# Two-layer attention kernel: softmax sums of one block interleaved with the folds of the block ahead

## Chip, cores, metric

The kernel runs on one core of a Trainium2 chip. The metric is device time in microseconds from start to end of the program. The engines are TensorE (PE, matrix products), VectorE (DVE), ScalarE (ACT), GpSimd (POOL) and SyncE (SP). Each has its own queue of instructions. SP and POOL also issue DMAs; a DMA that adds into its destination is issued from POOL.

## The reference

The input `x` is 16 images of 256 channels on 32 x 32 points, float32. Two layers with the same form run one after the other:

```python
def _conv_ref(x, Wq, bq, Wk, bk, Wv, bv, rel_h, rel_w):
    xf = x.reshape(b, c, n)                     # n = 1024, 4 heads of d = 64
    q, k, v = proj(Wq, bq), proj(Wk, bk), proj(Wv, bv)
    sim = jnp.einsum('bhdi,bhdj->bhij', q, k)
    rel = (rel_h + rel_w).reshape(heads, d, n)
    qpos = jnp.einsum('hdi,bhdj->bhij', rel, q)
    attn = jax.nn.softmax(sim + qpos, axis=-1)
    out = jnp.einsum('bhdn,bhmn->bhdm', v, attn)
    return out.reshape(b, c, w, h)

x = x + _conv_ref(_gn(x), *layer0)              # _gn: mean and variance over groups of the
x = x + _conv_ref(_gn(x), *layer1)              # last axis, 16 groups per image
```

## The kernel before

**Units and blocks.** A unit is one image in one layer; there are 32. A unit has four blocks: two pairs of heads (`pr`), and for each two halves of 512 columns (`half`). Blocks are numbered n = 0 to 127, and b = n mod 4 is called the position of a block in its unit here. `block(n)` issues positions 1 and 2, `block_with_q` position 0, `block_with_values` position 3, and `block_without_pieces` the last two blocks of all. The order of every instruction is written out by hand (`manual_schedule`); each engine takes its own instructions in that order.

**Inside a block.** A block has eight tiles of scores, j = 0 to 7. `seed` (VectorE, L442) writes the positional term into a PSUM tile, `scores` (TensorE, L478) adds the products of `k` and `q`, ScalarE takes the exponential into a tile `p` in SBUF (L487). There are four PSUM tiles (`ring`), one of which serves other products, and so a seed waits for the exponential that frees its tile. `attend` (L532) multiplies the eight `p` tiles with the values in two passes; the first score tile of the next block is computed between the passes. `take_out` (L594, ScalarE) copies the result at the end of each block. Beside this, every block carries pieces of the next unit's work: projections, values, positional terms and the normalisation.

**Normalisation.** `norms` spreads it over a unit in ScalarE activations per group: sums (`SUMS`) and squares for the unit two ahead, and the application (`norm_apply`, L248, from `APPLY`) for the next unit. The application starts in position 0. It needs `rstd` and `nshift`, which GpSimd computes (L237, L239) after VectorE has written `var` (L235) in position 3.

**The chain of softmax sums.** The denominator is the sum over all rows of the eight `p` tiles. For each block:

1. `add_up` (VectorE, L517 and L519) adds tiles 0 to 5 into `acc`, 128 x 1024. There are three `acc` buffers and ten `p` buffers.
2. `add_last` (GpSimd DMA, L550) adds tiles 6 and 7 in the next block: these 512 KB transfers are called chunks here. In position 2, VectorE adds tile 6 of the previous block itself.
3. `fold` (GpSimd DMA, L555) adds the lower half of the partitions to the upper.
4. `stack_up` (SP DMA, L569) copies 32 of the 64 rows into `stack`, and `fold_again` (GpSimd DMA, L574) adds the other 32. Two blocks with two heads each share one stack.
5. `fold_stack` (GpSimd DMA, L579) halves a stack five times: with D = 64, R = 32, R/2, R/4 and R/8 rows.
6. `spread_sums` (SP DMA, L587, four of them) brings the sums to `den_all`; `reciprocals` (VectorE, L629) inverts them and sends them through DRAM (L631, L636) to `rden`.
7. `normalise` (VectorE, L644) multiplies the block pair's result, and `add_by_dma` (GpSimd DMA, L662) adds it to `x`. `store` (SP, L667) writes `x` out after layer 1.

Before the change, steps 2 to 4 of block n-1 all run within block n, in series: each step waits for the DMA ahead of it. Steps 5 to 7 of a pair are spread over the blocks after it. In GpSimd's queue `fold_again` of position 2 stands, in position 3, ahead of `rstd`.

Of the kernel before, what the change touches and what calls it, by code (L numbers as in the profile page):

```python
# [13 lines left out]
ALU = mybir.AluOpType  # L14
# [5 lines left out]
G = 16  # L20
# [32 lines left out]
def fast_path(ctx, tc, sh, x, layers, out, W, den_all, good, flag):  # L53
# [26 lines left out]
    nc = tc.nc  # L80
# [464 lines left out]
    R = P // 4  # L545
    stacks = {}

    def add_last(blk, j0=NT - 1):
        for j in range(j0, NT):
            nc.gpsimd.dma_start(accs[blk], probs[blk, j], accum_op=ALU.add)  # L550

    def fold(blk):

        acc = accs[blk]
        nc.gpsimd.dma_start(acc[:D], acc[D:], accum_op=ALU.add)  # L555
# [20 lines left out]
    def fold_stack(u, pr, rows_):  # L576

        stack = stacks[u, pr]
        nc.gpsimd.dma_start(stack[:rows_], stack[rows_ : 2 * rows_], accum_op=ALU.add)  # L579
# [155 lines left out]


    APPLY = {0: (0, 1, 5, 9, 9), 1: (9, 9, 9, 11, G)}
    SUMS = {0: (0, 0, 0, 1, 7), 1: (7, 9, 11, G, G)}
    SQUARES = {2: (0, 0, 5, 11, G)}

    FIRST_SQUARES = {0: (3, 5, 9, G, G)}
# [2 lines left out]
    def norms(u, b, i):  # L744
# [9 lines left out]
        if u + 2 < NU:  # L754
            norm_squares(u + 2, groups(SQUARES))

    def block(n):
        blk = blocks[n]
        u, b = divmod(n, BPU)
        pr_, half = blk[1:]  # L760

        stacked = blocks[n - 3][:2] if half == 1 and n > 2 else None
        summed = blocks[n - 4][:2] if half == 0 and n > 3 else None
        last_unit = u + 1 == NU
        before = blocks[n - 5][:2] if b == 1 and n > 4 else None
# [8 lines left out]
        folded = n - 1 < FOLDED  # L774
# [7 lines left out]
        if previous and folded and b == 1:  # L782
            add_last(previous, NT - 2)
        elif previous:
            add_up(previous, 6)
            if folded:
                add_last(previous)
            else:
                add_up(previous, 7)
# [12 lines left out]
        add_up(blk, 1)  # L802
        if before:
            reciprocals(*before)
        norms(u, b, 1)
        second(0)
        if half == 1:
            second_out()
        if stacked:
            fold_stack(*stacked, D)  # L810
        if summed:
            fold_stack(*summed, R // 8)
            spread_sums(*summed)
        if previous and folded:
            fold(previous)
        if stacked:
            fold_stack(*stacked, R)
        first(1)
        first_out()
        seed(blk, 5, f0)  # L820
        scores(blk, 5)
        if previous and folded:
            stack_up(previous)
        if b == 2 and n > 5:
            store(*blocks[n - 6][:2])
        add_up(blk, 2)
# [32 lines left out]
        if stacked:  # L859
            fold_stack(*stacked, R // 2)  # L860
        if previous and folded:
            fold_again(previous)
        if half == 1 and u + 3 < NU and units[u + 3][1] == 0 and u > 0 or n == 3:
            load_x(units[u + 3][0], range(pr_, pr_ + 1) if u > 0 else range(CC))
        add_up(blk, 5)
        if n in (2, 6):
            W.mix(n // 4)
        if before and last_unit:
            finish(*before)
        if two and half == 1 or n == 0:  # L870
            mean_out()
        if stacked:
            fold_stack(*stacked, R // 4)
            if n == len(blocks) - 3:
                fold_stack(*stacked, R // 8)
                spread_sums(*stacked)
        if after:
            for j in range(1, 4):
                seed(after, j, ring[j % 3])
        if before and not last_unit:  # L880
            normalise(*before)
            add_by_dma(*before)
        norms(u, b, 3)
        values_of_p(1)
        take_out(blk, po)
        pos[n] = po

    def block_with_q(n):

        blk = blocks[n]  # L890
        u = blk[0]
        r0, r1, r2, r3 = ring
        previous, after, summed = blocks[n - 1], blocks[n + 1], blocks[n - 4][:2]
        folded = n - 1 < FOLDED
        before = blocks[n - 6][:2] if n > 5 else None
        add_last(previous, NT - 2)
# [11 lines left out]
        fold_stack(*summed, R // 8)  # L908
        spread_sums(*summed)
        fold(previous)  # L910
        first(1)
        first_out()
        seed(blk, 6, r0)
        scores(blk, 6)
        stack_up(previous)
        seed(blk, 7, r1)
        scores(blk, 7)
        add_up(blk, 2)
        add_up(blk, 3)
        seed(after, 0, r2)  # L920
        add_up(blk, 4)
        if n in check:
# [6 lines left out]
        fold_again(previous)  # L929
        ring[:] = r2, r0, r1, r3  # L930
        seed(after, 1, r0)
        seed(after, 2, r1)
        add_up(blk, 5)
        seed(after, 3, r2)
        if before:
            store(*before)
        norms(u, 0, 3)
        values_of_p(1)
        take_out(blk, po)
        pos[n] = po  # L940

    def block_with_values(n):
# [1 line left out]
        blk = blocks[n]  # L944
        u = blk[0]
        r0, r1, r2, r3 = ring
        previous, after, stacked = blocks[n - 1], blocks[n + 1], blocks[n - 3][:2]
        before = blocks[n - 5][:2] if n > 4 else None
        two = u + 2 < NU
        v = Values(u + 1, psum2(r3, f"pw_{u + 1}"))  # L950

        add_last(previous, NT - 2)
        scores(blk, 1)
        add_up(blk, 1)
        one = v.half(1, HI, False), v.half(1, LO, True)
# [13 lines left out]
        v.keep(1, 0, 1.0)  # L969
        seed(blk, 5, r2)  # L970
        scores(blk, 5)
        if before:
            reciprocals(*before)
        seed(blk, 6, r1)
        scores(blk, 6)
        v.combine(0, 0, ALU.add)
        fold_stack(*stacked, D)
        fold(previous)
# [5 lines left out]
        fold_stack(*stacked, R)  # L984
        stack_up(previous)
        add_up(blk, 2)
        seed(after, 0, r1)
        v.combine(1, 1, ALU.subtract)
# [12 lines left out]
        scores(after, 0)  # L1001
        v.pair("4", 3, 4, 1)
        v.keep(0, 1, -1.0)
        fold_stack(*stacked, R // 2)
        fold_again(previous)
        if u + 3 < NU and units[u + 3][1] == 0:
            load_x(units[u + 3][0], range(1, 2) if u > 0 else range(CC))
        add_up(blk, 4)
# [1 line left out]
            mean_out()  # L1010
        ring[:] = r1, r0, r3, r2
        seed(after, 1, r0)
        if before:
            normalise(*before)
        v.combine(1, 0, ALU.add)
        fold_stack(*stacked, R // 4)
        seed(after, 2, r3)
        if before:
            add_by_dma(*before)
        add_up(blk, 5)  # L1020
        seed(after, 3, r1)
        values_of_p(1)
# [517 lines left out]
```

## Time and profile before

| | us |
|---|---|
| median of 3 runs | 2757.56 (2753.45 to 2761.12) |
| profiled execution | 2760.36, span 2758.6 |
| granted TensorE clock, mean | 0.972 |
| VectorE adds into `acc` (L519), 550 | 669.7 |
| VectorE seeds (L442), 1018 | 1230.4, idle before them 322.2, of that 287.0 for exponentials |
| GpSimd chunk DMAs (L550), 217 of 512 KB | 6.0 median from issue to landing |
| GpSimd `stack<-acc` (L574) waiting for SP's `stack<-acc` | 422.2 |
| ScalarE exponentials waiting for a chunk DMA, 33 times | 51.4 |

A row of the profile's groups gives line, engine, operation, what is written from what, shape and count; then busy time and the mean of one in ns; then how long the engine stood idle just before such instructions, and which instruction ended most of that. In a timeline the columns are start, length, engine, line and operation, and in brackets the idle time before it. The granted clock is that of TensorE as a share of full speed. Matrix products are pipelined, so that a busy TensorE may still run slowly.

### The profile page before, as it was taken

The page shows a single profiled execution, that of the slowest core. Times are in us where ns is not written, and L with a number is a line of the kernel's source. Part 1 is how long each engine was busy: PE and PEld are TensorE (multiplying, and loading weights), DVE is VectorE, ACT ScalarE, POOL GpSimd, SP SyncE. Part 2 cuts the span into 40 slices and gives each one's busy share as a digit, 9 for nine tenths or more (in the row PEclk, how much of TensorE's full clock was granted, in tenths as well). Part 3 has the DMA queues.
Part 4 walks back from the last instruction along what each step waited for, and adds up shares of the span by engine and source line. Part 5 has one row for each costly group of instructions (what it writes and reads, how often), then busy time and mean ns, then how long its engine had stood idle before and what let it go on. Part 6 is the DMA issues. An engine that isn't in the chain of part 4 may idle for free. (4 is left out here: it accounts for less than half of the span.)

```text
span 2758.6 us, 94006 instructions
## 1 busy us (share of the span) xinstructions
PE 2599.2 (94%) x41192; PEld 1424.4 (52%) x41192; DVE 2233.9 (81%) x2184; ACT 2012.0 (73%) x3977; POOL 937.2 (34%) x1029
## 2 busy tenths in 40 slices
PE   8999999999999999999999999999999999999997
PEld 4555445554455554555545555445554455544554
DVE  7888777887877888788887788887887877878887
ACT  7877767778777786777776778777777776777653
POOL 1333333333333333333233332333323333333330
PEclk9999999999999999999999999999999999999999
DMA  3455555565556555655555556565556555555553
GB/s 95 92 99 107 103 103 107 109 132 115 114 113 120 105 111 108 119 110 113 120 103 114 108 109 117 109 124 114 113 120 118 109 104 108 108 98 109 109 109 83
DMA packets 141906, 302.32 MB, mean 110 GB/s; under 512 B 56361, under 2 KB 57897, under 8 KB 141489
## 3 DMA queue, kind: packets, MB, share of 16 engines
q0 software_dynamic: 75744, 210.33, 44.0%
q1 hardware_dynamic: 65744, 85.90, 11.2%
q8 instruction: 326, 5.34, 0.8%
q14 instruction: 92, 0.75, 0.1%
HBM read 51.78 MB, written 17.30 MB: 25 GB/s over the span
## 5 line engine op out<-in xcount | busy, mean ns | idle before, releaser
L442 DVE TENSOR_TENSOR ps<-abt 128x1024 f32<-128x1024 f32 x1018 | 1230.4, 1227 | 322.2 <-ACT p L487 287.0
L487 ACT ACTIVATE p<-ps,shift 128x1024 f32<-128x1024 f32 x993 | 1067.9, 1111 | 412.6 <-PE ps L478 355.4
L478 PE MATMUL ps<-q,k 64*64 64x512 f32 x7944 | 1003.6, 600 | 111.5 <-DVE ps L442 106.6
L532 PE MATMUL po<-p,v 64*64 64x256 f32 x16384 | 990.1, 390 | 26.5 <-ACT q L279 25.3
L532 PEld LDWEIGHTS po<-p,v 64*64 64x64 f32 x16384 | 661.2, 138 | 382.7 <-issue 91.4
L519 DVE TENSOR_TENSOR acc<-acc,p 128x1024 f32<-128x1024 f32 x550 | 669.7, 1218 | 4.8 <-ACT p L487 2.3
L478 PEld LDWEIGHTS ps<-q,k 64*64 64x64 f32 x7944 | 289.1, 133 | 521.8 <-DVE ps L442 259.8
L550 POOL DMA_DIRECT2D acc<-p x217 | 269.6, 1242 | 543.8 <-DMA acc<-p 219.2
L579 POOL DMA_DIRECT2D stack<-stack x310 | 301.8, 974 | 221.4 <-DMA stack<-stack 186.6
L574 POOL DMA_DIRECT2D stack<-acc x248 | 214.2, 985 | 454.7 <-DMA stack<-acc 422.2
L248 ACT ACTIVATE xn<-x,nshift,rstd 128x128 f32<-128x128 f32 x496 | 208.8, 493 | 132.8 <-POOL nshift L239 132.8
L555 POOL DMA_DIRECT2D acc<-acc x124 | 102.7, 828 | 508.7 <-DMA acc<-p 508.7
L268 PE MATMUL pk<-xn,Wk 64*64 64x512 f32 x2048 | 243.9, 592 | 0.0
L268 PE MATMUL pq<-xn,Wq 64*64 64x512 f32 x2048 | 242.8, 589 | 0.0
L517 DVE TENSOR_TENSOR acc<-p,p 128x1024 f32<-128x1024 f32 x128 | 156.7, 1224 | 92.5 <-ACT p L487 92.5
L190 ACT ACTIVATE junk<-x,neg 128x128 f32<-128x128 f32 x505 | 198.0, 400 | 0.0
L594 ACT COPY od<-po 128x512 f32<-128x512 f32 x127 | 74.2, 584 | 134.1 <-PE po L532 134.1
L268 PEld LDWEIGHTS pq<-xn,Wq 64*64 64x64 f32 x2048 | 77.8, 133 | 142.5 <-issue 133.8
L190 ACT ACTIVATE junk<-x 128x128 f32<-128x128 f32 x464 | 140.0, 310 | 0.0
L268 PEld LDWEIGHTS pk<-xn,Wk 64*64 64x64 f32 x2048 | 74.2, 134 | 125.3 <-issue 123.3
L363 PEld LDWEIGHTS pw<-mixed,t 64*64 64x64 f32 x2976 | 114.3, 133 | 38.3 <-DVE v L405 20.4
L363 PE MATMUL pw<-Wv,xn 64*64 64x128 f32 x1984 | 133.6, 273 | 0.3 <-issue 0.3
(96 smaller groups left out, 1932.3 us busy)
## 6 DMA issues: line engine op xcount, KB each, us to landing
acc<-p POOLq DMA_DIRECT2D x217, 512.0 KB, 6.0
rden<-rd SPq DMA_DIRECT2D x126, 256.0 KB, 4.8
acc<-acc POOLq DMA_DIRECT2D x124, 256.0 KB, 3.5
x<-od POOLq DMA_DIRECT2D x61, 512.0 KB, 4.9
x<-in_x_dram SPq DMA_DIRECT2D x32, 512.0 KB, 4.0
stack<-acc SPq DMA_DIRECT2D x248, 64.0 KB, 2.1
stack<-acc POOLq DMA_DIRECT2D x248, 64.0 KB, 2.9
out_dram<-x SPq DMA_DIRECT2D x31, 512.0 KB, 3.0
```

Of the source, the lines that this page charges most:

```text
L190: nc.scalar.activation(junk, grouped(xt[units[u][0]], g), func, accum_out=into[:, g : g + 1], **bias)
L248: nc.scalar.activation(grouped(xns[u], g), grouped(xt[units[u][0]], g), AF.Identity, bias=shift[:, g : g + 1], scale=rstd[:, g : g + 1],)
L268: yield nc.tensor.matmul(pk[c, nh, :], w[l][rs, cc, c0 : c0 + D], xns[u][rs, cc, nh * HALF : (nh + 1) * HALF], start=(t == 0 and cc == 0), ...
L363: yield nc.tensor.matmul(self.pw[c, a, part * P : (part + 1) * P], x[rs, j0 : j0 + D], w[rs, :], start=first and not whole and part == 0, ...
L442: nc.vector.tensor_tensor(ps.rearrange("p h (w y) -> p h w y", y=H), ab[:, :, :H].unsqueeze(2).to_broadcast([P, 2, XH, H]), ab[:, :, H + h ...
L478: nc.tensor.matmul(ps[c, h, :], a[hs, j0 : j0 + D], b[hs, columns], start=bool(tag) and i == 0, stop=i == len(terms) - 1, skip_group_check ...
L487: nc.scalar.activation(p, ps, AF.Exp, bias=W.shift)
L519: nc.vector.tensor_tensor(accs[blk], accs[blk], probs[blk, j], ALU.add)
L532: yield nc.tensor.matmul(po[c, a, :QUART], vts[u][rs, pr, j, h * D : (h + 1) * D], p[rs, h, a * QUART : (a + 1) * QUART], start=(t == 0 an ...
L550: nc.gpsimd.dma_start(accs[blk], probs[blk, j], accum_op=ALU.add)
L574: nc.gpsimd.dma_start(at, acc[R:D, h, :], accum_op=ALU.add)
L579: nc.gpsimd.dma_start(stack[:rows_], stack[rows_ : 2 * rows_], accum_op=ALU.add)
```

## The change

The sums of a block now take two blocks instead of one. A new function `denominators(n, i)` holds all steps of the chain, in slots i = 0 to 4 of a block, and the three kinds of block call it. In block n the chunks of block n-1 are added, while the folds (steps 3 and 4) are those of block n-2, and the stack and the spread come a block later than before. The chunks of tiles 6 and 7 are now added by DMA in every position, and VectorE no longer adds tile 6 in position 2. For positions 0 and 2, VectorE's add of tile 5 moves to the start of the next block. `reciprocals` moves from before seed 5 to before seed 6 in position 1, and from before seed 6 to after seed 7 in position 3. `normalise` and `add_by_dma` move from the end of positions 1 and 3 to the start of positions 2 and 0 (`residual`). `store` stays in positions 0 and 2, now behind the residual of the same block. One group of `SUMS` moves from the third to the fourth slot of position 0. The order on TensorE is the same as before.

```diff
-    def add_last(blk, j0=NT - 1):
-        for j in range(j0, NT):
-            nc.gpsimd.dma_start(accs[blk], probs[blk, j], accum_op=ALU.add)
+    def add_chunk(blk, j):
+        nc.gpsimd.dma_start(accs[blk], probs[blk, j], accum_op=ALU.add)
...
-    SUMS = {0: (0, 0, 0, 1, 7), 1: (7, 9, 11, G, G)}
+    SUMS = {0: (0, 0, 0, 0, 7), 1: (7, 9, 11, G, G)}
...
+    def denominators(n, i):
+
+        half, end = n % 2, n == FOLDED
+        if n > FOLDED + 1:
+            return
+        previous, older = blocks[n - 1], blocks[n - 2]
+        folding = n <= FOLDED and n > 1
+        stacked = blocks[n - 4][:2] if half == 0 and n > 3 else None
+        summed = blocks[n - 5][:2] if half == 1 and n > 4 else None
+        late = blocks[n - 3][:2] if n == FOLDED + 1 else None
+        if i == 0:
+            if n > 0 and n % BPU in (1, 3):
+                add_up(previous, 5)
+            if end or n > FOLDED:
+                add_up(previous, 6)
+            if n > FOLDED:
+                add_up(previous, 7)
+            elif n > 0:
+                add_chunk(previous, 7 if end else 6)
+            if summed:
+                fold_stack(*summed, R // 8)
+                spread_sums(*summed)
+            if stacked:
+                fold_stack(*stacked, D)
+            if folding:
+                fold(older)
+        elif i == 1:
+            if late:
+                fold_stack(*late, D)
+            if stacked:
+                fold_stack(*stacked, R)
+            if n > 0 and n < FOLDED:
+                add_chunk(previous, 7)
+            elif end:
+                fold(previous)
+            if folding:
+                stack_up(older)
+                fold_again(older)
+        elif i == 2:
+            if late:
+                fold_stack(*late, R)
+            if summed:
+                reciprocals(*summed)
+            if stacked:
+                fold_stack(*stacked, R // 2)
...
+        elif i == 3:
...
+            if stacked:
+                fold_stack(*stacked, R // 4)
...
+    def residual(n):
+        if n > 5:
+            normalise(*blocks[n - 6][:2])
+            add_by_dma(*blocks[n - 6][:2])
...
     def block(n):
...
+        denominators(n, 0)
+        if b == 2:
+            residual(n)
...
         add_up(blk, 1)
-        if before:
-            reciprocals(*before)
...
         seed(blk, 5, f0)
         scores(blk, 5)
-        if previous and folded:
-            stack_up(previous)
+        add_up(blk, 2)
+        denominators(n, 2)
...
     def block_with_q(n):
...
-        add_last(previous, NT - 2)
+        after = blocks[n + 1]
+        denominators(n, 0)
+        residual(n)
...
     def block_with_values(n):
...
-        stack_up(previous)
+        denominators(n, 2)
         add_up(blk, 2)
```

`FOLDED` is 124, the number of blocks whose sums go this way; the last four are treated apart (`end`, `late`), some of their sums staying on VectorE and TensorE.

More of the change, by code (lines that the diff above doesn't have):

```diff
@@ L755, in norms @@
             norm_squares(u + 2, groups(SQUARES))
+    def denominators(n, i):
[42 more added lines that the diff above has]
+                fold_stack(*stacked, R // 2)
+            if end:
+                stack_up(previous)
+        elif i == 3:
+            if late:
+                fold_stack(*late, R // 2)
+            if stacked:
+                fold_stack(*stacked, R // 4)
+            if end:
+                fold_again(previous)
+        elif late:
+            fold_stack(*late, R // 4)
+            fold_stack(*late, R // 8)
+            spread_sums(*late)
+    def residual(n):
+        if n > 5:
+            normalise(*blocks[n - 6][:2])
+            add_by_dma(*blocks[n - 6][:2])
     def block(n):
@@ L760, in block @@
         pr_, half = blk[1:]
-        stacked = blocks[n - 3][:2] if half == 1 and n > 2 else None
-        summed = blocks[n - 4][:2] if half == 0 and n > 3 else None
         last_unit = u + 1 == NU
-        before = blocks[n - 5][:2] if b == 1 and n > 4 else None
         after = blocks[n + 1] if n + 1 < len(blocks) else None
@@ L773, in block @@
         f0, f1, f2, f3 = ring
-        folded = n - 1 < FOLDED
         if not pieces:
@@ L780, in block @@
             return block_with_values(n)
-        if previous and folded and b == 1:
-            add_last(previous, NT - 2)
[L784 to L789, printed above, removed]
+        denominators(n, 0)
+        if b == 2:
+            residual(n)
         if b == 2:
@@ L808, in block @@
             second_out()
[L809 to L813, printed above, removed]
-        if previous and folded:
-            fold(previous)
-        if stacked:
-            fold_stack(*stacked, R)
+        denominators(n, 1)
         first(1)
@@ L821, in block @@
         scores(blk, 5)
-        if previous and folded:
-            stack_up(previous)
+        add_up(blk, 2)
+        denominators(n, 2)
         if b == 2 and n > 5:
             store(*blocks[n - 6][:2])
-        add_up(blk, 2)
         if b == 2:
@@ L858, in block @@
             mean_out = norm_var(1, filled(f1, f"pm_{n}", EPS / 2))
[L859 to L862, printed above, removed]
+        denominators(n, 3)
         if half == 1 and u + 3 < NU and units[u + 3][1] == 0 and u > 0 or n == 3:
             load_x(units[u + 3][0], range(pr_, pr_ + 1) if u > 0 else range(CC))
-        add_up(blk, 5)
+        if b == 1:
+            add_up(blk, 5)
         if n in (2, 6):
             W.mix(n // 4)
-        if before and last_unit:
-            finish(*before)
         if two and half == 1 or n == 0:
             mean_out()
[L872 to L876, printed above, removed]
+        denominators(n, 4)
         if after:
@@ L879, in block @@
                 seed(after, j, ring[j % 3])
-        if before and not last_unit:
-            normalise(*before)
-            add_by_dma(*before)
+        if b == 1 and last_unit:
+            finish(*blocks[n - 5][:2])
         norms(u, b, 3)
@@ L892, in block_with_q @@
         r0, r1, r2, r3 = ring
[L893 to L896, printed above, removed]
+        after = blocks[n + 1]
+        denominators(n, 0)
+        residual(n)
         for j in range(1, 4):
@@ L907, in block_with_q @@
         add_up(blk, 1)
-        fold_stack(*summed, R // 8)
-        spread_sums(*summed)
-        fold(previous)
+        denominators(n, 1)
         first(1)
@@ L928, in block_with_q @@
         scores(after, 0)
-        fold_again(previous)
+        denominators(n, 3)
         ring[:] = r2, r0, r1, r3
[L931 to L936, printed above, removed]
+        for j in range(1, 4):
+            seed(after, j, ring[j % 3])
+        if n > 5:
+            store(*blocks[n - 6][:2])
         norms(u, 0, 3)
@@ L946, in block_with_values @@
         r0, r1, r2, r3 = ring
-        previous, after, stacked = blocks[n - 1], blocks[n + 1], blocks[n - 3][:2]
-        before = blocks[n - 5][:2] if n > 4 else None
+        after = blocks[n + 1]
         two = u + 2 < NU
         v = Values(u + 1, psum2(r3, f"pw_{u + 1}"))
-        add_last(previous, NT - 2)
+        denominators(n, 0)
         scores(blk, 1)
@@ L971, in block_with_values @@
         scores(blk, 5)
-        if before:
-            reciprocals(*before)
         seed(blk, 6, r1)
@@ L976, in block_with_values @@
         v.combine(0, 0, ALU.add)
-        fold_stack(*stacked, D)
-        fold(previous)
+        denominators(n, 1)
         v.pair("3", 5, 7, 0)
@@ L983, in block_with_values @@
         v.keep(1, 1, -1.0)
-        fold_stack(*stacked, R)
-        stack_up(previous)
+        denominators(n, 2)
         add_up(blk, 2)
@@ L1003, in block_with_values @@
         v.keep(0, 1, -1.0)
-        fold_stack(*stacked, R // 2)
-        fold_again(previous)
+        denominators(n, 3)
         if u + 3 < NU and units[u + 3][1] == 0:
@@ L1012, in block_with_values @@
         seed(after, 1, r0)
-        if before:
-            normalise(*before)
         v.combine(1, 0, ALU.add)
-        fold_stack(*stacked, R // 4)
         seed(after, 2, r3)
-        if before:
-            add_by_dma(*before)
         add_up(blk, 5)
```

## The prediction

> **Where the time goes now.** I read the busy shares first, then the groups for who waits for whom, then block by block, then one block in order of time. The page's first part:
>
> ```profile
> PE 2599.2 (94%) x41192; PEld 1424.4 (52%) x41192; DVE 2233.9 (81%) x2184; ACT 2012.0 (73%) x3977; POOL 937.2 (34%) x1029
> ```
>
> TensorE is busy 94% of the span, 159 us short of all of it. But "busy" hides slow products, and the groups say where to look:
>
> ```profile
> L478 PE MATMUL ps<-q,k 64*64 64x512 f32 x7944 | 1003.6, 600 | 111.5 <-DVE ps L442 106.6
> L248 ACT ACTIVATE xn<-x,nshift,rstd 128x128 f32<-128x128 f32 x496 | 208.8, 493 | 132.8 <-POOL nshift L239 132.8
> ```
>
> PE waits almost only for score seeds from VectorE (106.6 us). ScalarE waits 132.8 us for GpSimd's `nshift`, in 29 waits, one per unit. To see whether these are one thing I cut the span at the ScalarE copies that end each block (L594) and took busy time and granted clock of such stretches. First come blocks 48 to 51 (positions 0 to 3 of a unit), then the four blocks of unit 1, then block 61:
>
> ```profile
> 1041.63:1068.07 26.44, 21.02 (x228) 9.11 (x224) 18.17 (x16) 15.69 (x33) 12.19 (x12) 0.87 0.57 110
> 1068.07:1086.33 18.26, 18.26 (x300) 9.06 (x296) 15.94 (x17) 16.32 (x36) 4.35 (x5) 1.00 0.56 110
> 1086.33:1107.03 20.70, 20.70 (x260) 9.61 (x256) 18.98 (x18) 17.43 (x44) 8.44 (x10) 1.00 0.54 94
> 1107.03:1128.70 21.67, 21.54 (x516) 16.24 (x512) 17.27 (x19) 14.19 (x16) 5.95 (x7) 1.00 0.69 141
> 109.16:127.29 18.13, 17.63 (x228) 8.43 (x224) 16.57 (x15) 15.52 (x34) 3.62 (x5) 1.00 0.45 81
> 1317.83:1340.56 22.73, 20.52 (x300) 9.30 (x296) 16.03 (x17) 16.55 (x36) 5.34 (x7) 0.92 0.59 124
> ```
>
> The columns are length, busy time of PE, weight loads, VectorE, ScalarE and GpSimd, then clock, DMA share and GB/s. Position 0 takes 26.44 us where the same work took 18.13 in unit 1; positions 1 to 3 run full. Over units 2 to 30 the means are 23.49, 18.98, 21.05 and 21.89 us: 85.4 a unit, against 78.8 in unit 1. Position 0 also loses clock (0.86 to 0.93 in 25 of 29, 1.00 in 4). GpSimd, ScalarE and TensorE in block 48 show why:
>
> ```profile
> 1046.64 1.71 POOL L574 DMA_DIRECT2D stack<-acc  x2 [1.13 <-issue]
> 1047.77 4.30 POOL L237 TENSOR_TENSOR rstd<-var,mhalf 128x16 f32<-128x16 f32 x1
> 1052.14 0.22 POOL L239 TENSOR_TENSOR nshift<-neg,rstd 128x16 f32<-128x16 f32 x1
> ...
> 1052.40 0.49 ACT L248 ACTIVATE xn<-x,nshift,rstd 128x128 f32<-128x128 f32 x1 [5.28 <-POOL nshift L239]
> ...
> 1055.21 1.45 PE L478 MATMUL ps<-q,k 64*64 64x512 f32 x8 [3.31 <-DVE ps L442]
> ...
> 1057.48 6.20 PE L532 MATMUL po<-p,v 64*64 64x256 f32 x64 [0.82 <-ACT q L279]
> ```
>
> `rstd` is ready to be computed before block 48 begins (VectorE writes `var` some 6 us before a position 3 ends) but sits in GpSimd's queue behind `fold_again`, whose accumulating DMA waits for the whole chain of the block before: chunk 6, chunk 7, fold, stack. ScalarE stands 5.28 us at `xn`; the exponentials behind it free no PSUM, the seeds come late, PE stops 3.31 us, and the next products take 6.20 us where the second half takes 3.62. So the chain of sums, which nobody needs soon, bounds position 0 through queue order.
>
> **The `rstd` pair.** After: in position 3 the queue holds chunk 6, R/8 fold, fold of the older block, chunk 7, `fold_again` of the older block, then `rstd`. The older block's chunks landed a block ago, so only three waits are left: chunk 7 for chunk 6 (landing median 6.0 us), the stacking behind the spread on SP, `fold_again` for it. That gives about +13.3 us into position 3; `var` comes at +15.9, `nshift` 4.2 us later at +20.1, and ScalarE reaches `xn` at about +25. Hidden with 5 us to spare. Position 0 should take unit 1's 18.13; I take 18.2. Gain (23.49 - 18.2) x 29 = **154 us**. What is late next there? VectorE gets `normalise` (1.22 us) moved in, before seed 4, which slips by 0.6 us to +3.8; scores 4 start at +4.2. Covered, barely. Its operand is ready: reciprocal at +10 of position 3 plus 7.8 us of two DMAs (1325.4 to about 1333 in block 61).
>
> **Adds moved to DMA.** 550 to 520 at L519, 217 to 247 at L550. 30 x 1.218 = 37 us off VectorE, worth nothing directly where PE is full; it removes the small seed waits of positions 2 and 3 (21.05 to 20.7, 21.89 to 21.7): 0.55 x 29 = **16 us**. The 30 more DMAs: queue 0 spent 44.0% of 2758.6 us on 210.33 MB, 5.8 us per MB, so 3.0 us each, 91 us in all, 3% of the span on top of a DMA share of about 55%; GpSimd issues them in 30 x 1.24 us at 34% busy. Nothing, as long as no one waits for the last chunk, which lands about +13 into a block whose buffers are wanted again some 6 us later.
>
> **Add 5 moved over the boundary** (positions 0 and 2). VectorE sits idle 3.08 us at the start of blocks 49 and 51, so the 1.22 us fits. But chunk 6 must wait for it, and the R/8 fold is queued behind chunk 6.
>
> **The new wait.** Before, R/8 and the spread ran at the end of position 0, and the reciprocal stood before seed 5 of position 1. Now all of this starts in position 1, and the reciprocal stands before seed 6. Blocks 60 and 61 (GpSimd, SP, VectorE) show the same chain, running late there (the last chunk, the R/8 fold, the four spreading DMAs, the reciprocal):
>
> ```profile
> 1313.24 0.85 POOL L550 DMA_DIRECT2D acc<-p  x1 [5.89 <-DMA acc<-p]
> 1313.78 1.16 POOL L579 DMA_DIRECT2D stack<-stack  x1
> ...
> 1320.05 2.90 SPq L587 DMA_DIRECT2D den_all<-stack  x4
> ...
> 1325.40 0.25 DVE L629 RECIPROCAL r<-den_all 128x16 f32<-128x16 f32 x1 [2.09 <-DMA den_all<-stack]
> ```
>
> R/8 to the spread: 6.3 us here, 4.4 to 4.6 in most position 0 blocks; spread to reciprocal, in six blocks where it waited, 3.7 to 5.8, mean 4.7. In the new order add 5 ends at +0.1 of position 1, chunk 6 issues at +0.2, R/8 at +0.75, spread at +5.2, reciprocal at **+9.9** (8.9 to 11.7). VectorE is there at +6.6. Seed 6 then ends at +11.3; PE finished scores 5 at +8.45: a gap of 2.9 us. Behind the reciprocal are seeds 6 and 7, adds 3 and 4, the next block's seeds, and PE waits for them all. Position 3 has the same chain, but there the reciprocal follows seed 7, and VectorE arrives at about +9.8: hidden.
>
> What does 2.9 us cost? The Trainium skill (TensorE: Matmul & The Clock Gate, HAM oscillation) says to avoid PE gaps over about 3.4 us; by that 2.9 keeps the clock and position 1 takes 18.26 + 2.9 = 21.2, a loss of 2.2 x 30 = 67 us, and the whole gains 103. The rows here disagree: position 0 blocks whose longest gap was 2.75 to 2.8 us had 0.86 to 0.93, and block 122 had 0.93 after 2.15. One step of 0.07 is 1.7 us of a block, two are 3.4. I take the rows: 2.0 more, 23.2 us, near block 61's 22.73 (idle 2.2, clock 0.92). Loss (23.2 - 18.98) x 30 = **127 us**. Bounds: 20.2 us (reciprocal at +8.9, no step) costs 37; 26.4 (at +11.7, two steps) costs 223.
>
> The same skill (DMA: Bandwidth & Descriptors, Anatomy of one DMA) fits a GpSimd DMA as 2.0 us + bytes/436e3: 3.2 us for chunk 6. The row says 6.0 median, 4.9 at best (R/8 lands with it). By the rule the reciprocal would come 1.7 us earlier and the gap be 1.2. The transfers here accumulate; I take the row.
>
> **Other steps**, all about nothing: ScalarE's 33 waits on chunk DMAs (51.4 us) vanish, their cost being in the means above; one group sum moves a few us later in position 0, under ScalarE idle; the accumulators have three buffers and `fold_again` lands at +15 of the block before reuse; x<-od moves from a block's end to the next one's start, landing before its readers; stores and loads on SP follow it with 10 us to spare; the last four blocks change by a few us either way.
>
> **Sum.** 154 + 16 - 127 = 43 us. The profiled execution took 2760.36 us (span 2758.6): 2717. The median of the runs is 2.8 lower: **2715 us**.
>
> **Rivals.** (B) The den chain is quick, reciprocal by +9, clock kept: position 1 at 21.2, T = 2655. For it: 4.4 + 3.7 us, the quickest of each leg, make +8.9, and queue 0 holds only chunk 6 then. Against: it takes the quick end of both legs at once. (C) Slower: R/8 also waits for the R/4 fold, the end of a chain of landings (chunk 6, D, R, R/2, R/4) that I put at +17.2 of position 0. Shortening that block to 18.2 takes its slack. If R/4 lands 1.6 us into position 1, the reciprocal is at +11.5, gap 4.5, two steps, 26.2 us: 217 lost, T = 2757.6 + 47 = 2805. It decides once position 1 passes 18.98 + 170/30 = 24.65, a gap of 3.0 with two steps or 4.7 with one. (D) The change does not free `rstd`: if stacking slips behind the spread by over 7 us in position 3, half the 154 stays lost: 2792.
>
> **How the numbers follow.** Chances: forecast (2670 to 2755) 0.48, B 0.22, C 0.20, D 0.10. A measurement of this kernel tells 0.3% (8 us) from no change. Faster: 0.87 of the first and all of B, 0.64. Same: 0.09, from the edges of the first, C and D. Slower: 0.27. The range 2640 to 2800 takes in B and nearly all of C; the forecast's own is 2670 to 2755.
>
> **What would show it.** Right: the `xn` wait on `nshift` near zero; position 0 at 18.2 with clock 1.00; a wait of about 3 us at the reciprocal in position 1 alone, that block near 23 with clock about 0.9; R/8 issued about 0.7 us into it. Wrong: position 0 still over 21, or a reciprocal that waits under 2 us or over 5.

## The result, and the profile after

The changed kernel takes 2899.73 us, median of 4 runs (2894.66 to 2910.35), beside 2755.51 us for the kernel before on the same chip: a ratio of 1.053, 95% interval 1.049 to 1.057. The forecast was a gain of 43 us; it became a loss of 144. The profiled span grew from 2758.6 to 2895.2 us, by 136.6, and the mean granted clock fell from 0.972 to 0.960.

From the page of the changed kernel, the busy shares and then the groups (columns as before):

```profile
PE 2602.7 (90%) x41192; PEld 1406.5 (49%) x41192; DVE 2197.2 (76%) x2154; ACT 2023.2 (70%) x3977; POOL 1005.9 (35%) x1059
...
L478 PE MATMUL ps<-q,k 64*64 64x512 f32 x7944 | 1034.5, 620 | 205.1 <-DVE ps L442 200.0
...
L628 DVE RECIPROCAL r<-den_all 128x16 f32<-128x16 f32 x64 | 16.1, 252 | 288.8 <-DMA den_all<-stack 288.8
L248 ACT ACTIVATE xn<-x,nshift,rstd 128x128 f32<-128x128 f32 x496 | 210.9, 500 | 0.0
```

The same wait of the reciprocal in the kernel before (total us, times, longest):

```profile
DVE r L629 <- DMA den_all<-stack: 18.1, 13, 5.2
```

The wait of `xn` for `nshift` is gone: 0.0 where it was 132.8 us. In its place the reciprocal waits 288.8 us for the sums, where it waited 18.1 before, and PE's waits for seeds rose from 106.6 to 200.0 us. VectorE is busy 37 us less; most of the fall of its share from 81% to 76% is the longer span.

Cut into blocks 60 to 63 (positions 0 to 3 of a unit), the changed kernel shows where:

```profile
1370.14:1388.27 18.13, 17.62 (x228) 8.28 (x224) 17.57 (x16) 15.58 (x33) 7.78 (x9) 1.00 0.82 160
1388.27:1414.58 26.31, 20.26 (x300) 9.56 (x296) 16.09 (x18) 16.61 (x36) 8.59 (x10) 0.87 0.64 131
1414.58:1435.22 20.64, 20.64 (x260) 9.16 (x256) 17.91 (x17) 17.45 (x43) 5.93 (x7) 1.00 0.47 79
1435.22:1458.98 23.76, 22.06 (x516) 16.64 (x512) 16.17 (x19) 14.22 (x17) 10.16 (x8) 1.00 0.53 115
```

Position 0 runs at the 18.13 us of an undisturbed block. Position 1 takes 8 us more than 18.26, with its clock down to 0.87, and position 3 about 2 more. Also new is a DMA share of 0.82 in position 0 (on average 0.77 there, 0.50 before). The means over units 2 to 30:

| position | before | forecast | after | change x 29 |
|---|---|---|---|---|
| 0 | 23.49 us, clock 0.90 | 18.2 | 18.14, 1.00 | -155 us |
| 1 | 18.98, 1.00 | 23.2 | 27.18, 0.87 | +238 |
| 2 | 21.05, 1.00 | 20.7 | 20.64, 1.00 | -12 |
| 3 | 21.89, 1.00 | 21.7 | 24.18, 1.00 | +66 |

The changes add up to 137 us, as much as the difference of the spans. Twenty-five of 29 position 0 blocks had a clock below 0.97 before, none has now; in position 1 it is all 29 now, against one.

Blocks 60 and 61 of the changed kernel in order of time (GpSimd's queue from the R/2 fold on, then SP, VectorE and PE; block 61 begins at 1388.27):

```profile
1384.09 0.83 POOL L573 DMA_DIRECT2D stack<-acc  x1 [3.98 <-issue]
1385.78 0.83 POOL L573 DMA_DIRECT2D stack<-acc  x1 [0.86 <-DMA stack<-acc]
1386.32 1.12 POOL L578 DMA_DIRECT2D stack<-stack  x1
1389.19 0.81 POOL L578 DMA_DIRECT2D stack<-stack  x1 [1.75 <-DMA stack<-stack]
1389.99 0.95 POOL L549 DMA_DIRECT2D acc<-p  x1
1391.75 0.81 POOL L578 DMA_DIRECT2D stack<-stack  x1 [0.81 <-DMA stack<-stack]
...
1397.00 3.23 SPq L586 DMA_DIRECT2D den_all<-stack  x4
...
1401.48 0.25 DVE L628 RECIPROCAL r<-den_all 128x16 f32<-128x16 f32 x1 [6.57 <-DMA den_all<-stack]
1401.65 2.34 DVE L442 TENSOR_TENSOR ps<-abt 128x1024 f32<-128x1024 f32 x2
...
1402.91 3.69 PE L478 MATMUL ps<-q,k 64*64 64x512 f32 x16 [6.05 <-DVE ps L442]
```

This is the chain that the forecast named, with the same links, and late from its first. `fold_again` holds R/2 back to the last 2 us of position 0; R/4 waits for R/2 and is issued 0.9 us into position 1. Chunk 6 stands behind R/4 in GpSimd's queue and is issued at +1.7, not +0.2; R/8 waits for R/4 and is issued at +3.5, not +0.75. The spread follows at +8.7 and the reciprocal at +13.2, after VectorE has stood still for 6.57 us. The seeds stand behind it, and PE gets nothing for 6.05 us.

The view of DMA issues of the changed kernel (size of each, median us from issue to landing):

```profile
acc<-acc POOLq DMA_DIRECT2D x124, 256.0 KB, 6.1
...
stack<-acc SPq DMA_DIRECT2D x248, 64.0 KB, 3.5
...
stack<-stack POOLq DMA_DIRECT2D x62, 64.0 KB, 5.6
den_all<-stack SPq DMA_DIRECT2D x248, 2.0 KB, 3.9
```

The same view of the kernel before:

```profile
acc<-acc POOLq DMA_DIRECT2D x124, 256.0 KB, 3.5
...
stack<-acc SPq DMA_DIRECT2D x248, 64.0 KB, 2.1
...
stack<-stack POOLq DMA_DIRECT2D x62, 64.0 KB, 3.3
den_all<-stack SPq DMA_DIRECT2D x248, 2.0 KB, 2.6
```

Their sizes did not change; what is in flight beside them did. Chunk 6, a D fold, a fold and the residual add are now issued within 2 us at the start of position 0. Not every landing grew: the chunks went from 6.0 to 5.2 us and R/8 from 5.3 to 4.4, and R/2 and R/4 kept theirs (2.5 to 2.7 and 2.4 to 2.3).

### The profile page after: what moved, and what is told of

Same layout as the page of the kernel before. It is cut to its first block, busy times and chain, and to the rows that moved or that the text cites. A ratio compares the mean times of both kernels' runs of the same rounds, so it can differ in the third digit from the quotient of the medians.

```text
span 2895.2 us, 94108 instructions
## 1 busy us (share of the span) xinstructions
PE 2602.7 (90%) x41192; PEld 1406.5 (49%) x41192; DVE 2197.2 (76%) x2154; ACT 2023.2 (70%) x3977; POOL 1005.9 (35%) x1059
## 4 chain that ended last, share of the span: by engine, by line
PE 38%; DMA 29%; DVE 11%; issue 10%; SPq 5%; POOL 4%; ACT 2%; DVEq 0%; POOLq 0%; ACTq 0%
PE po L532 14%; PE ps L478 14%; DMA stack<-stack 11%; DMA den_all<-stack 7%; DMA acc<-acc 7%; DVE acc L519 5%; SPq L586 5%; DMA stack<-acc 4%; PE pq L268 4%; PE pk L268 4%; DVE ps L442 3%; POOL acc L549 2%; POOL stack L573 1%; DVE v L405 1%; ACT p L487 1%
## 5 line engine op out<-in xcount | busy, mean ns | idle before, releaser
L442 DVE TENSOR_TENSOR ps<-abt 128x1024 f32<-128x1024 f32 x1018 | 1223.8, 1228 | 190.6 <-ACT p L487 136.6
L478 PE MATMUL ps<-q,k 64*64 64x512 f32 x7944 | 1034.5, 620 | 205.1 <-DVE ps L442 200.0
L532 PE MATMUL po<-p,v 64*64 64x256 f32 x16384 | 955.6, 381 | 15.6 <-ACT q L279 15.2
L532 PEld LDWEIGHTS po<-p,v 64*64 64x64 f32 x16384 | 638.2, 135 | 372.1 <-issue 80.7
L519 DVE TENSOR_TENSOR acc<-acc,p 128x1024 f32<-128x1024 f32 x520 | 633.0, 1217 | 2.9
L549 POOL DMA_DIRECT2D acc<-p x247 | 256.5, 1039 | 607.2 <-ACT od L593 273.3
L578 POOL DMA_DIRECT2D stack<-stack x310 | 312.1, 1007 | 263.6 <-DMA stack<-stack 246.4
L628 DVE RECIPROCAL r<-den_all 128x16 f32<-128x16 f32 x64 | 16.1, 252 | 288.8 <-DMA den_all<-stack 288.8
L554 POOL DMA_DIRECT2D acc<-acc x124 | 172.4, 1391 | 1.1 <-issue 1.1
L237 POOL TENSOR_TENSOR rstd<-var,mhalf 128x16 f32<-128x16 f32 x31 | 122.7, 3958 | 111.8 <-DVE var L235 111.8
L363 PE MATMUL pw<-mixed,t 64*64 64x128 f32 x2976 | 136.6, 272 | 3.4 <-issue 1.9
```

The source lines that it names most:

```text
L442: nc.vector.tensor_tensor(ps.rearrange("p h (w y) -> p h w y", y=H), ab[:, :, :H].unsqueeze(2).to_broadcast([P, 2, XH, H]), ab[:, :, H + h ...
L478: nc.tensor.matmul(ps[c, h, :], a[hs, j0 : j0 + D], b[hs, columns], start=bool(tag) and i == 0, stop=i == len(terms) - 1, skip_group_check ...
L519: nc.vector.tensor_tensor(accs[blk], accs[blk], probs[blk, j], ALU.add)
L532: yield nc.tensor.matmul(po[c, a, :QUART], vts[u][rs, pr, j, h * D : (h + 1) * D], p[rs, h, a * QUART : (a + 1) * QUART], start=(t == 0 an ...
```

## The experiments

Three theories stand in the expectations. **W**: the loss is the reciprocal's wait in position 1. **A**: it is add 5 over the boundary, which holds back chunk 6 and with it R/8. **L**: it is the load of 30 more chunk DMAs. A time without a ratio is that of one execution, beside which the kernel before had medians of 2752.6 to 2759.7 us; a ratio has its 95% interval. Times with a plus or minus count from the start of the block, and are means over units 2 to 30 where no block is named.

### Is it the wait at the reciprocal?

**`d1_recip_const`** takes the reciprocal of a constant tile, so that it waits for no sum (the normalisation by the real sums is left out):

```diff
-        nc.vector.reciprocal(r8[:, :count, :], den_all[:, n : n + count, :])
+        src = den_all[:, n : n + count, :]
+        if n < FOLDED:
+            src = W.large.rearrange("p (x e) -> p x e", e=8)
+        nc.vector.reciprocal(r8[:, :count, :], src)
```

> The changed kernel, but up to block 123 the reciprocal inverts a constant tile (1e24) and not den_all, so the normalisation is left out; the spread, the folds, all DMAs and the order of every engine stay. Theory W (the reciprocal's wait for den_all, ahead of seeds 6 and 7 in position 1 and of the value sums in position 3, costs everything): position 1 falls from 27.1 to about 18.3 us, position 3 from 24.2 to 21.8, the unit from 90.1 to 79, time about 2900 - 29.5 x 11.1 = 2570 us. Rival L (30 more chunk DMAs and the crowding of the DMA queue slow the kernel): these are all still there, so 2850 us or more. Rival A (add 5 moved over the boundary holds VectorE): also still there, 2850 or more.

It took 2702.86 us. Position 1 fell from 27.2 to 18.25 us, so the wait is the whole loss there. Position 3 fell from 24.2 to 22.5, with a median of 21.7: the wait is most of the loss. Ten of its 29 blocks still take 22.6 to 26.3 us; in two of them, blocks 27 and 63, PE stops for 2.4 and 2.9 us with nothing in the profile that it waits for. And position 2 rose from 20.6 to 24.8, which the expectation had missed. The waits of this kernel (total us, times, longest):

```profile
DVE od L646 <- DMA rden<-rd: 126.5, 30, 8.0
```

The DMAs that carry the reciprocals to `rden` still stand in SP's queue behind the spread and the stack, and `normalise` now waits for them.

**`e1_recip_slot3`** keeps the whole new chain and every GpSimd instruction in order. The reciprocal goes one slot later, behind seed 7, and the residual behind add 1 in position 0 and behind `second_out` in position 2:

```diff
         elif i == 2:
...
-            if summed:
-                reciprocals(*summed)
...
         elif i == 3:
+            if summed:
+                reciprocals(*summed)
...
     def block_with_q(n):
...
         denominators(n, 0)
-        residual(n)
...
         add_up(blk, 1)
+        residual(n)
         denominators(n, 1)
```

> The changed kernel with the reciprocal moved to slot 3 (in position 1 behind seed 0 of the next block, in position 3 behind its seed 0 as well) and normalise behind add 1 of positions 2 and 0; GpSimd's order stays. Theory W: VectorE reaches the reciprocal at about +12.6 where it is ready at +13.2, so position 1 is 18.3 to 19.5 us, position 3 about 22, position 0 18.2, position 2 20.7 to 21.5: 2755 - 29.5 x 5 to 6 = 2575 to 2610 us, under both kernels. Rival L: the crowding stays, 2800 us or more. If the later reciprocal only moves the wait to normalise in position 2, position 2 rises to 23 or more and the time is about 2660.

It took 2608.28 us (2606.28 to 2616.68), 0.947 of the kernel before (0.944 to 0.950), and so beats both kernels. Blocks 60 to 63, and VectorE in block 61 (from 1250.89):

```profile
1232.77:1250.89 18.12, 18.07 (x228) 8.25 (x224) 17.64 (x16) 15.54 (x33) 7.75 (x9) 1.00 0.81 158
1250.89:1269.15 18.26, 18.26 (x300) 9.61 (x296) 13.91 (x16) 16.33 (x37) 6.68 (x8) 1.00 0.52 94
1269.15:1290.04 20.89, 20.87 (x260) 9.57 (x256) 19.89 (x19) 17.42 (x43) 6.99 (x9) 1.00 0.79 161
1290.04:1311.84 21.80, 21.67 (x516) 16.84 (x512) 16.07 (x19) 14.20 (x17) 10.94 (x9) 1.00 0.54 103
```

```profile
1262.22 1.23 DVE L442 TENSOR_TENSOR ps<-abt 128x1024 f32<-128x1024 f32 x1
1263.40 0.09 DVE L202 MEMSET pm<- 128x32 f32 x1
1265.80 0.25 DVE L628 RECIPROCAL r<-den_all 128x16 f32<-128x16 f32 x1 [2.32 <-DMA den_all<-stack]
1265.97 1.16 DVE L519 TENSOR_TENSOR acc<-acc,p 128x1024 f32<-128x1024 f32 x1
```

The reciprocal is no earlier (14.9 us into the block, on average 14.75) and still waits, 2.32 us here; but seed 7 is already out, and PE is full through the block. Positions 2 and 3 take 21.6 and 22.4 us on average, against 20.6 and 24.2 in the changed kernel. The chain was never too slow for its reader. It was too slow for the place in VectorE's queue at which the reader stood.

### Is it add 5?

**`d3_add5_home`** puts add 5 back into its own block in positions 0 and 2:

```diff
         if i == 0:
-            if n > 0 and n % BPU in (1, 3):
-                add_up(previous, 5)
...
-        if b == 1:
-            add_up(blk, 5)
+        add_up(blk, 5)
...
         seed(after, 1, r0)
         seed(after, 2, r1)
+        add_up(blk, 5)
         seed(after, 3, r2)
```

> The changed kernel with add 5 of positions 0 and 2 back in its own block, all else kept. Theory W: the R/8 fold waits for the R/4 fold and not for chunk 6, so the reciprocal comes less than 1 us sooner: 2870 to 2900 us. Rival A: chunk 6 and R/8 come 1 to 3 us sooner in positions 1 and 3, or VectorE gains its idle start: 2800 us or less.

It took 2817.93 us. Both theories hold, each for one position. Position 3 fell from 24.2 to 21.9 us: R/8 is issued 3.3 us before the block instead of 1.2 into it, and VectorE, there at about +9.9, no longer waits. Position 1 stayed at 26.9: chunk 6 there stands behind the issue of R/4 and not behind add 5 (+1.9 us instead of +2.1), and R/8 waits for R/4.

**`e2_slot3_add5_home`** is `e1_recip_slot3` with this edit as well.

> The version with the reciprocal in slot 3 (2608 us), with add 5 of positions 0 and 2 back in its own block. Theory W: add 5 at home took position 3 of the changed kernel from 24.2 to 21.9 us, most of it by letting the reciprocal come before it is wanted; here the reciprocal is hidden already and position 3 stands at 22.15, of 21.7 possible: 2590 to 2608 us. VectorE's idle 3 us at the start of positions 1 and 3 are left unused, and if that costs more, 2610 to 2640.

2610.43 us (2606.62 to 2618.42), ratio 0.948 (0.945 to 0.951): the same as without. Where no seed stands behind the wait for the sums, the place of add 5 costs nothing.

### Why the chain is late in position 1

**`d5_stack_folds_ahead`** moves R/2 and R/4 from slots 2 and 3 to slot 1, ahead of `stack_up` and `fold_again`; **`d6_ahead_and_home`** adds the edit of `d3_add5_home`.

```diff
         elif i == 1:
...
+            if stacked:
+                fold_stack(*stacked, R // 2)
+                fold_stack(*stacked, R // 4)
             if folding:
                 stack_up(older)
                 fold_again(older)
...
-            if stacked:
-                fold_stack(*stacked, R // 2)
...
-            if stacked:
-                fold_stack(*stacked, R // 4)
```

> The changed kernel with the R/2 and R/4 folds issued ahead of fold_again in positions 0 and 2 (they wait for the R fold, not for it). Theory W, with the cause put at the R/4 fold: in the changed kernel R/4 issues 0.9 us into position 1, behind fold_again, so R/8 is at +3.5 and the reciprocal at +13.2. Here R/4 has landed before position 1 starts, R/8 follows chunk 6 at about +0.9, the reciprocal comes at about +10.5, position 1 falls from 27.1 to about 23.5 us, position 3 stays: 2900 - 30 x 3.6 = 2790 us. Rival A (add 5 and chunk 6 hold R/8): no gain in position 1, 2880 or more. Rival L: no gain.

> The last kernel with add 5 back in its own block as well. In the changed kernel add 5 alone at home left position 1 at 26.8 us (R/8 waits for R/4) and took position 3 from 24.2 to 21.9. Theory W: with R/4 early, add 5 at home now counts in position 1 too, R/8 goes out about 1 us before the block and the reciprocal comes at about +8.5 to 9.5: position 1 at 20 to 22.5 us, position 3 at 21.8, 2755 - 29.5 x (85.4 - 81.9) = about 2650 us (2620 to 2700). If position 1 is held by something else than this chain, 2750 or more.

2885.28 and 2812.14 us: both misses. In the first, R/4 was issued at -1.0 us of position 1 instead of +1.6 and R/8 at +2.2 instead of +4.3, but the spread only 1.0 us earlier (+7.3) and the reciprocal 0.6 us earlier (+13.15). The landings tell why. In the traces of all the kernels here, a GpSimd DMA that was issued while an earlier one was in flight always landed after it, in over 10,000 such pairs. R/8 stands behind chunk 6 in the queue and landed after it here too. Chunk 6 went out only 1.0 us sooner (+1.2 instead of +2.1) and landed at +6.6 instead of +7.3, and the spread, which waits for R/8, followed.

**`d9_no_r8_fold`** leaves the R/8 fold out, spreads rows not fully summed and caps the reciprocals, so that the normalisation is not computed:

```diff
+        nc.vector.tensor_scalar(r8[:, :count, :], r8[:, :count, :], 1e-24, None, ALU.min)
...
             if summed:
-                fold_stack(*summed, R // 8)
                 spread_sums(*summed)
```

> The changed kernel without the R/8 folds: den_all holds incomplete sums, and the reciprocals are capped at 1e-24, so the normalisation is left out. The spread then waits for the R/4 fold and no longer for a fold queued behind chunk 6. Theory W, with the wait priced link by link: R/4 goes out 0.9 us into position 1 and lands at about +3.4, spread at +3.5, reciprocal at +8 (13.2 with the R/8 fold). VectorE is there at +6.7, so it waits 1.3 us; position 1 takes 18.3 + about 1 = 19 to 20.5 us, position 3 21.8 to 22.5 us: 2900 - 30 x (7.3 + 1.9) = about 2625 us. If the reciprocal's wait is not what fills position 1, the time stays over 2800.

2793.28 us, far from the expectation. The spread began at +4.0 instead of +8.3, 4.3 us sooner, and the reciprocal came at +11.6 instead of +13.75, 2.1 us sooner: four 2 KB DMAs and their flight, 5.5 us in the changed kernel, took 7.6 us when they ran beside chunk 6 and the fold. Half of what the cut link gave was lost again in the spread; that these neighbours are the reason is not shown.

**`d11_no_xod`** leaves out the residual add `x<-od` (so `x` is never updated), the largest transfer in the bunch:

```diff
             normalise(*blocks[n - 6][:2])
-            add_by_dma(*blocks[n - 6][:2])
+            outs.pop(blocks[n - 6][:2])
```

> The changed kernel without the 512 KB DMA x<-od (the residual isn't added, 60 transfers fewer); the order of all else stays. In the changed kernel position 0 issues chunk 6, the D fold, the fold and x<-od within 2 us of each other, and the R fold behind them lands after 5.6 us where it took 3.3 before. Theory P (the pile-up in GpSimd's DMA queue stretches the landings that R/4 waits for): the R fold lands about 3 us sooner, R/4 goes out at -1 and not +1.6 of position 1, R/8 at +2, the reciprocal at +11.5 and not +13.75, position 1 25 and not 27.1 us: about 2835 us. If the chain is set by its links one after another and not by the pile-up, R/4 and the reciprocal stay within 1 us of where they are and the time is 2870 or more.

2862.93 us. From the view of DMA issues of this kernel:

```profile
stack<-stack POOLq DMA_DIRECT2D x62, 64.0 KB, 2.5
```

The R fold, issued right behind `x<-od` in the changed kernel, lands in 2.5 us instead of 5.6; R/4 is issued 1.8 us sooner, the reciprocal comes 1.5 us sooner (+12.26), and position 1 takes 25.7 us. So the bunching at the start of position 0 is shown as a cause of 1.5 us of the delay.

### The parts of the change on the kernel before

**`d2_rstd_first`**: the kernel before, with the two GpSimd folds of position 3 put behind `rstd`.

```diff
-        fold_stack(*stacked, R // 2)
-        fold_again(previous)
...
             mean_out()
+        fold_stack(*stacked, R // 2)
+        fold_again(previous)
```

> The kernel before with one edit: in position 3 the R/2 fold and fold_again are issued after the rstd pair and not ahead of it. It takes the queue order alone. Theory W: ScalarE's 132.8 us at nshift go, position 0 falls from 23.5 to about 18.2 us, the rest keeps, 2755 - 29 x 5.3 = 2600 us. If position 0 was bound by something else (the two chunks in series, the late p buffers), 2700 us or more. A part may come back in position 1, where the chain of sums runs on: up to 40 us.

2689.56 us (2675.76 to 2693.72), ratio 0.974 (0.970 to 0.978). Its waits:

```profile
ACT p L487 <- DMA acc<-p: 114.6, 60, 6.3
...
ACT xn L248 <- POOL nshift L239: 7.0, 5, 2.8
```

The wait for `nshift` goes from 132.8 to 7.0 us and position 0 from 23.5 to 18.9; but position 1 goes from 19.0 to 21.1. There ScalarE waits 51.1 us for the `p` buffers of chunks, which stand behind the moved folds, where it waited 16.2 before; and the reciprocal's wait rises from 18.1 to 43.7 us in all. The two moved instructions alone bring 2.6%.

**`d7_chunk_only`**: the kernel before, with tile 6 of every position 1 block also added by DMA.

```diff
-        if previous and folded and b == 1:
+        if previous and folded and b in (1, 2):
             add_last(previous, NT - 2)
```

> The kernel before with one part of the change: tile 6 of position 1's block is added by DMA in position 2 and not by VectorE, so 31 more 512 KB DMAs and 31 fewer VectorE adds. Theory W: the DMAs cost next to nothing by themselves, 2735 to 2775 us. Rival L: 31 transfers crowd the queue, 2800 us or more.

2946.43 us, 194 more than before. The waits of this kernel:

```profile
ACT p L487 <- DMA acc<-p: 234.0, 113, 10.1
ACT xn L248 <- POOL nshift L239: 234.0, 29, 9.9
```

It is not load: the changed kernel carries about as many chunks, and its positions 0 and 2 run full. In the serial chain one chunk more makes `rstd` 4.3 us later in GpSimd's queue, and position 0 takes 27.1 us instead of 23.5: 104 us in all. Positions 2 and 3 take 1.1 and 1.4 us more, and there ScalarE waits 168.7 us for chunks, where it waited 25.5.

**`d8_before_two_moves`**: `d2_rstd_first` with the reciprocal of position 1 behind seed 7. **`d10_rd_ahead_of_stack`**: the same, with `stack_up` of that block issued behind the reciprocal.

```diff
-        if before:
-            reciprocals(*before)
...
         scores(blk, 7)
+        if before:
+            reciprocals(*before)
```

```diff
-        if previous and folded:
+        if previous and folded and not before:
             stack_up(previous)
...
             reciprocals(*before)
+            if folded:
+                stack_up(previous)
```

> The kernel before with rstd ahead of the R/2 fold and fold_again in position 3 (2690 us alone) and the reciprocal of position 1 behind seed 7. Alone the first left position 1 at 21.2 us, with the reciprocal ready at about +7.8 us ahead of seed 5. Theory W: the reciprocal is hidden behind the seeds (VectorE gets there at +8.9), position 1 falls to 18.3 to 19 us: 2690 - 30 x 2.5 = 2615 us. If position 1 is held by ScalarE's waits for the last chunk's buffer, as the rows of that run also show (50 us in 27 waits), it stays above 20 us and the time near 2660.

> The kernel before with both moves of the run at 3003 us, where SP issued the reciprocal's rd and rden behind stack_up of the same block, and this waited for the fold until 1.4 us into position 2; normalise then waited 9.8 us for rden. Here that stack_up is issued behind rd and rden. If SP's queue order made that run slow: rd goes out at +9.2 of position 1, rden lands at about +17, position 2 falls from 34.7 to 21 to 22 us, and the time to about 3003 - 30 x 13 = 2610 us (2590 to 2680, as stack_up comes later for the chain behind it). If the late reciprocal itself was the reason, it stays over 2850.

3003.01 us (2992.78 to 3008.9; ratio 1.093, 1.089 to 1.096) and 2691.43 us. SP and VectorE of `d8_before_two_moves` around block 62 (from 1443.44):

```profile
1444.83 1.11 SPq L569 DMA_DIRECT2D stack<-acc  x2
1445.99 0.57 SPq L631 DMA_DIRECT2D rd<-r  x1
1447.72 1.12 SPq L636 DMA_DIRECT2D rden<-rd  x2
...
1452.72 1.23 DVE L644 TENSOR_TENSOR od<-od,rden 128x1024 f32<-128x1024 f32 x1 [9.82 <-DMA rden<-rd]
```

Moving the reciprocal moved its two steps of DMA behind `stack_up` in SP's queue, and `stack_up` waits for the fold, into the next block. `normalise` waited 356.3 us in all and position 2 took 34.7 us. In `d10_rd_ahead_of_stack`, where only that order differs, the wait is 32.4 us and position 2 takes 22.2. That version is as fast as `d2_rstd_first` and no faster: exponentials still wait 137.6 us for chunks. `e1_recip_slot3`, whose chain has a block more of time, is another 83 us faster, and its exponentials wait 5.3 us for chunks.

## Why the prediction was wrong, point by point

- **The `rstd` pair: right.** Forecast 18.2 us and 154 us gained; measured 18.14 and 155, no wait at `xn`, clock 1.00.
- **Adds moved to DMA, for nothing: right of the load, wrong of the company.** Positions 0 and 2 run full with these chunks. But I priced every landing of the new chain from rows in which DMAs follow each other in series. In the new order four kinds of them take half as long again or more, the R fold and the spread among them.
- **Add 5, and "Position 3 ... hidden": wrong by its size.** VectorE arrived as forecast (+10.2, forecast +9.8), the reciprocal at +12.74 and not +9.9: R/8 0.5 us later, its landing 0.8 longer, the spread's 1.5 longer. `d3_add5_home` shows that the late start of chunk 6 makes the difference between waiting and not. 66 us instead of a gain of 6.
- **The new wait: right in place and mechanism, mis-sized. This is the term that failed:** "R/8 at +0.75, spread at +5.2, reciprocal at +9.9". Measured means are +4.3, +8.3 and +13.75 (the last from 12.4 to 16.0). VectorE waited 7.1 us on average, over the 5 us that I had named as a sign of being wrong. By the times of issue 3.5 of these 3.85 us are R/8's, which I let wait for chunk 6 alone; it waits for R/4, which I had landing inside position 0 and which is issued at +1.6 of position 1. Chunk 6 itself, which I had at +0.2, stands behind that issue and goes out at +2.1, though add 5 ends at +0.1 as forecast. But `d5_stack_folds_ahead` and `d6_ahead_and_home` bring R/8 to +2.2 and +2.0 and the reciprocal only to +13.1: with R/8 nearer to its forecast time, the two legs behind it take 11.0 us where I had 9.15 from serial rows: 5.1 for 4.45 to the spread, since R/8 lands behind chunk 6, and 5.9 for 4.7 from there. So both assumptions fail together, the order that I read and the landings that I took. The step from lateness to time held: block 61 is 18.26 + 6.05 idle + 2.0 for the clock = 26.31 us, and the mean of position 1 is 18.26 + 6.6 + 2.3, where I had 2.9 of gap and 2.0 for the clock: 4.0 us over the forecast for a reciprocal 3.85 later. My upper bound, 26.4 us, had no place for R/4 nor for longer landings.
- **Rival C** named the cause, "R/8 also waits for the R/4 fold", and I gave it 0.20 and a reciprocal at +11.5. It put the loss in position 1 at 217 us, where 238 were measured; the rest of its miss is position 3.
- **The clock gate.** A gap of 5.2 to 8.8 us is beyond both the Trainium skill's 3.4 us (TensorE: Matmul & The Clock Gate, HAM oscillation) and the shorter gaps of the rows, and all 29 blocks lost clock, so position 1 does not decide between them. The traces do elsewhere. In the kernel before, all 20 blocks of units 2 to 30 whose longest gap was 2.0 to 3.4 us were granted 0.86 to 0.93, as the rows said. In the other kernels 30 of 64 such blocks were granted less than 0.97, so the longest gap alone does not settle it; from 4 us on all 232 were.

Shown: that the waits at the reciprocal are the loss in position 1 (238 us, `d1_recip_const`) and in position 3 (66 us, `d3_add5_home`); that the bunch at the start of position 0 makes 1.5 us of the lateness, and add 5 that of position 3; that with the reciprocal one slot later, and the residual behind it, a loss of 5.3% becomes a gain of 5.3%. Undone with little effect: R/8's wait for R/4, whose landing ended it in 27 of 29 blocks of the changed kernel and in one of `d5_stack_folds_ahead`. Undone only in part: chunk 6 behind R/4 or `fold_again` in GpSimd's queue (+0.8 in `d6_ahead_and_home` and +0.9 in `d11_no_xod`, not the +0.2 of the forecast). Not isolated: which neighbour lengthens the flight of the spread.

## What to carry to other kernels

When a chain of DMAs is shifted, time it from its first late link, with the landings that they will have beside their new neighbours, and not with medians from a serial order. Then ask for the latest place in the reader's in-order queue at which nobody behind it waits: one slot for the reciprocal, and the residual with it, was worth 291 us here, and no quickening of the chain came near. And follow a moved instruction's own DMAs into their queue; the same move cost some 310 us in `d8_before_two_moves` for standing behind one waiting issue.

## What the runs showed of the hardware

- A 64 KB accumulating DMA landed in 5.6 us when issued right behind the 512 KB residual add, and in 2.5 us without it. GpSimd's DMAs landed in the order of their issue in every pair that was in flight together, over 10,000 in 14 traces; a stack fold issued behind a 512 KB chunk landed 0.15 us or more after it in all 1,759 cases. The 2 KB spreads went from 2.6 to 3.9 us at a mean DMA rate of only 110 GB/s over the span. The share of busy DMA engines over a span did not tell of it; that of one position did (0.77 in position 0, 0.50 before).
- Starting the spread 4.3 us sooner brought the reciprocal behind it only 2.1 us sooner (`d9_no_r8_fold`).
- One chunk DMA more per unit in the serial chain cost 194 us for 31 of them (`d7_chunk_only`, one execution), although the engines that move them were busy for 55% of the span.
